# Keeping four engines in program order beside a stream of gathers

## The chip, the cores and the metric

The kernel runs on one core of one Trainium2 chip. The metric is the device time of one execution, in microseconds; lower is better. Each run was timed beside the kernel before on the same chip. The median of the kernel before in the first measurements was 12008.74 us (3 runs; with a fourth, timed beside the changed kernel, 12002.22).

A ratio here is the mean time of one kernel's fast runs over that of the other's in the same rounds. It is therefore not quite the ratio of the medians that are quoted beside it.

## The reference

The input has 4 images of 256 channels and 64 x 64 pixels, in float32. Four layers follow each other, each with a group normalisation in front and a residual sum behind. What matters here is in layer 0:

```python
t = depthwise3x3(y)                                  # per channel
offset, mask = einsum(t, off_w), softmax(einsum(t, mask_w))
sg = 2.0 * (loc + offset / norm) - 1.0               # where to look, 9 points x 4 groups per pixel
samp = _grid_sample(img, sg)                         # bilinear: 4 neighbours of each point
dout = (samp * mask).sum(-1)                         # the "sampling"
dout = einsum(dout, outproj_w) + outproj_b
... # squeeze-excite and a feed-forward of 1024 channels
# layer 1: linear attention with 5x5 depthwise "taps"; layer 2: binarised 3x3 conv; layer 3: attention
```

The sampling reads data-dependent rows of a table in device memory. Everything else is dense arithmetic.

## The kernel before

Each image goes through *prepare*, then *sample*, then *first* (feed-forward and layer 1), then *second* (layers 2 and 3). The sampling of one image runs beside *first* and *second* of earlier images. The sampling is written like this:

```python
RP, UR, BR = 14, 4, 20            # 14 pixels a round, 4 rounds a unit, 20 rounds a block
...
for u in range(0, len(rounds), UR):
    unit = rounds[u:u + UR]
    wm = self.gp.tile([P, UR, 4 * G, OB], F32, name="wm")
    self.tc.keep_in_program_order(nc.vector.tensor_tensor(wm[:, 0:nu], ...))   # weights of the unit
    acc = self.ps1.tile([P, UR, P], F32, name="acc")
    for v, (r, m) in enumerate(unit):
        g = self.gp.tile([P, G, 256], F32, name="g", bufs=10)      # ring of 10 buffers
        for i in range(G):
            nc.gpsimd.indirect_dma_start(out=g[:, i, :], ..., in_=table, ...)   # 4 gathers a round
        for x in range(2):
            for i in range(G):                                     # 8 matmuls a round, 32 columns each
                nc.tensor.matmul(acc[32 * i:32 * i + 32, v, :], wm[:, v, ...],
                                 g[:, i, x * P:(x + 1) * P], start=x == 0, stop=x == 1)
    at = sp.tile([P, UR, P], F32, name="at", bufs=1)
    nc.scalar.copy(at[:, 0:nu], acc[:, 0:nu])                      # accumulator to SBUF
    dp = self.ps1.tile(...)
    for v in range(nu):
        nc.tensor.transpose(dp[:, v]..., at[:, v], self.ident)     # then dT <- dp on ScalarE
    ...
    yield 1                                                        # one step a unit
```

The work beside is a set of Python generators. After each step of the sampling, `beside` advances them by their share of a budget. An order written in this way is only a wish: the framework's scheduler decides at build time how the instructions stand in each engine's queue.

Of the kernel before, what the change touches and what calls it, by code (L numbers as in the profile page):

```python
# [1 line left out]

# [33 lines left out]
PREPARE = NB * 20 + NCH * 45  # L36
FIRST = NB * 28 + 2 * (NB * 10 + NCH * 56) + NB * 8 + NCH * 96
SECOND = 2 * NB * 16 + NB * 6 + NT * 9
# [27 lines left out]
class Net:  # L66
# [34 lines left out]
    def groupnorm(self, pool, st, name):  # L101

        nc = self.nc
        mv = pool.tile([P, KT, 2], F32, name=name + "_mv")
        for k in range(KT):
            nc.vector.bn_aggr(mv[:, k, :], st[:, k].rearrange("p b s -> p (b s)"))
        pg = self.ps(name + "_pg")
        nc.tensor.matmul(pg[:, 0:KT], self.bd8, mv[:, :, 0], start=True, stop=True)
        mg = pool.tile([P, KT], F32, name=name + "_mg")
        nc.vector.tensor_copy(mg, pg[:, 0:KT])  # L110
        d = pool.tile([P, KT], F32, name=name + "_d")
        nc.vector.tensor_tensor(d, mv[:, :, 0], mg, ALU.subtract)
        nc.vector.tensor_tensor(d, d, d, ALU.mult)
        nc.vector.tensor_tensor(d, d, mv[:, :, 1], ALU.add)
        pv = self.ps(name + "_pv")
        nc.tensor.matmul(pv[:, 0:KT], self.bd8, d, start=True, stop=True)
        sc = self.rsqrt(pool, pv[:, 0:KT], EPS_GN, KT, name)
        bi = pool.tile([P, KT], F32, name=name + "_bi")
        nc.vector.scalar_tensor_tensor(bi, mg, -1.0, sc, ALU.mult, ALU.mult)
        return sc, bi  # L120
# [41 lines left out]
    def depthwise(self, acc, src, w, k, rows, cols, r0, bias=None):  # L162

        nc = self.nc
        for t in range(k * k):
# [6 lines left out]
            else:  # L172
                nc.vector.tensor_scalar(acc, s, wt, None, ALU.mult)

# [92 lines left out]
    def prepare(self, n, w, sp, bp):  # L267
# [8 lines left out]
        sc, bi = self.groupnorm(sp, st, "g0")  # L276
# [4 lines left out]
        nc.vector.tensor_scalar(low, sh, SLOPE, None, ALU.mult)  # L281

# [14 lines left out]
        for b in range(NB):  # L297
# [5 lines left out]
            for m in range(KT):  # L303
# [4 lines left out]
                self.spread([p[:, m] for p in pads], rw(yb[:, m]), b, 1)  # L308
            nc.sync.dma_start(self.y_d[n][:, :, b * 512:(b + 1) * 512], yb)
# [5 lines left out]
            for j2 in range(2):  # L315
                ps = self.ps().rearrange("p (j o) -> p j o", o=C)
                for j in range(2):
                    at = (2 * j2 + j) * P
                    for k in range(KT):
                        nc.tensor.matmul(ps[:, j], yb[:, k, at:at + P], w["iw"][:, k], start=k == 0, stop=k == KT - 1)  # L320
                nc.vector.tensor_tensor(xo[:, 2 * j2:2 * j2 + 2, :], ps,
                                        self.row("inproj_b").unsqueeze(1).to_broadcast([P, 2, C]), ALU.add)
            for r in range(2):
# [6 lines left out]
            yield 17 - 2 * (b == 0)  # L330
# [27 lines left out]
    def offsets(self, n, c, y, mw, bp):  # L358
# [3 lines left out]
        for k in range(KT):  # L362
            acc = self.ps1.tile([P, 16, W], F32, name="agg", tag="agg")
            self.depthwise(acc, y[:, k], self.w3[:, k], 3, 16, W, 0, bias=self.sh[:, 2 + k:3 + k])
            nc.scalar.activation(t[:, k], acc.rearrange("p r w -> p (r w)"), AF.Identity, scale=SLOPE)
            nc.vector.tensor_tensor(t[:, k], acc.rearrange("p r w -> p (r w)"), t[:, k], ALU.max)
            yield 14
# [11 lines left out]
        self.coordinates(bp, n, c, off, ml)  # L379
        yield 17  # L380

    def coordinates(self, bp, n, c, off, ml):
# [27 lines left out]
            self.con("gi").rearrange("p (g q) -> p g q", q=PT).unsqueeze(1).to_broadcast([P, CT, G, PT]), ALU.add)  # L410

# [5 lines left out]
        nc.scalar.activation(mg, mg, AF.Exp)  # L417
        nc.vector.tensor_reduce(mx, mg, AX.X, ALU.add)
        nc.vector.reciprocal(mx, mx)
        nc.vector.tensor_tensor(mg, mg, bc(mx), ALU.mult)  # L420
        mf = ml.rearrange("p t q -> p (t q)")
        wt = sd[:, :, :, G:].rearrange("p t q (g a b) -> p t g q a b", g=G, a=2)
        for xt, wx in ((0, w0[:, 0]), (1, loc[:, 0])):
# [6 lines left out]
            sd.rearrange("p t q f -> p t (q f)"))  # L430


    def sample(self, n, ssum):


        nc, sp = self.nc, self.sp2
        table = self.tab[n].rearrange("g y x s c -> (g y x) (s c)")
        for b, (p0, np_) in enumerate(BLOCKS):
            sl = sp.tile([P, BR, G * 5], F32, name="sl")
            whole, part = np_ // RP, np_ % RP  # L440

            nr = whole + (part > 0)
            rows = self.s_d[n][p0 * PT:p0 * PT + nr * RS, :].rearrange("(r p) f -> p r f", p=RS)
# [3 lines left out]
            yb = sp.tile([P, KT, BP], F32, name="yb", bufs=1)  # L447
            nc.sync.dma_start(yb[:, :, 0:np_], self.y_d[n][:, :, p0:p0 + np_])
            dT = sp.tile([P, G, BP], F32, name="dT", bufs=1)
            rounds = [(r, RP) for r in range(whole)] + [(whole, part)] * (part > 0)  # L450
            for u in range(0, len(rounds), UR):
                unit = rounds[u:u + UR]
                nu = len(unit)

                wm = self.gp.tile([P, UR, 4 * G, OB], F32, name="wm")
                sh = [P, nu, 4 * G, OB]

                self.tc.keep_in_program_order(nc.vector.tensor_tensor(  # L458
                    wm[:, 0:nu], self.con("own").unsqueeze(1).unsqueeze(1).to_broadcast(sh),
                    sl[:, u:u + nu, G:].unsqueeze(3).to_broadcast(sh), ALU.mult))  # L460
                acc = self.ps1.tile([P, UR, P], F32, name="acc")
                for v, (r, m) in enumerate(unit):
                    g = self.gp.tile([P, G, 256], F32, name="g", bufs=10)
                    for i in range(G):
                        nc.gpsimd.indirect_dma_start(  # L465
                            out=g[:, i, :], out_offset=None, in_=table,
                            in_offset=bass.IndirectOffsetOnAxis(ap=sl.bitcast(I32)[:, r, i:i + 1], axis=0))


                    for x in range(2):  # L470
                        for i in range(G):
                            nc.tensor.matmul(acc[32 * i:32 * i + 32, v, :], wm[:, v, 4 * i + 2 * x:4 * i + 2 * x + 2, :],  # L472
                                             g[:, i, x * P:(x + 1) * P], start=x == 0, stop=x == 1)
                at = sp.tile([P, UR, P], F32, name="at", bufs=1)
                nc.scalar.copy(at[:, 0:nu], acc[:, 0:nu])  # L475
                dp = self.ps1.tile([P, UR, G, 2, OB], F32, name="dp", tag="dp")
                for v in range(nu):
                    nc.tensor.transpose(dp[:, v].rearrange("p g s o -> p (g s o)"), at[:, v], self.ident)  # L478

                full = sum(1 for _, m in unit if m == RP)  # L480
                for v0, v1, m in ((0, full, RP), (full, nu, unit[-1][1])):
                    for s in range(2):
                        if v0 < v1:
                            hs = slice(64 * s, 64 * s + 64)
                            q0 = RP * (u + v0)
                            nc.scalar.copy(
                                dT[hs, :, q0:q0 + m * (v1 - v0)].rearrange("p g (v o) -> p g v o", o=m),
                                dp[hs, v0:v1, :, s, 0:m].rearrange("p v g o -> p g v o"))
                yield 1
            for m in range(KT):  # L490
                po = self.ps1.tile([P, 512], F32, name="po", tag="dp")
                for k in range(G):
                    nc.tensor.matmul(po[:, 0:np_], self.ow[:, k, m * P:(m + 1) * P], dT[:, k, 0:np_], start=k == 0, stop=k == G - 1)  # L493
                ym = yb[:, m, 0:np_]
                nc.vector.tensor_tensor(ym, po[:, 0:np_], ym, ALU.add)  # L495
                nc.scalar.activation(ym, ym, AF.Identity, bias=self.sh[:, 4 + m:5 + m],
                                     scale=self.inv[:, 4 + m:5 + m], accum_out=ssum[:, m, b:b + 1])
            nc.sync.dma_start(self.x2_d[n][:, :, p0:p0 + np_], yb[:, :, 0:np_])


    def feedforward(self, n, ssum, st):
        nc, tc, a = self.nc, self.tc, self.a
        with tc.tile_pool(name=f"fa{n}", bufs=1, side="right") as sp, \
# [16 lines left out]
            nc.scalar.activation(dn, ps[0:64, 0:1], AF.Relu, bias=self.vec("se_down_b")[0:64])  # L520
            ex = sp.tile([P, KT], F32, name="ex")
# [5 lines left out]
            for k in range(KT):  # L527
                nc.scalar.activation(f1[:, k], f1[:, k], AF.Identity, scale=ex[:, k:k + 1])
            for b in range(NB):
# [3 lines left out]
                for m in range(4 * KT):  # L533
# [4 lines left out]
                    if m % 2:  # L538
                        yield 3.5
                for m in range(KT):  # L540
# [4 lines left out]
                    yield 7  # L545
# [4 lines left out]
    def layer1(self, n, st, st2):  # L550
# [3 lines left out]
        with tc.tile_pool(name=f"la{n}", bufs=1, side="right") as sp, \  # L554
# [5 lines left out]
            sc, bi = self.groupnorm(sp, st, "g1")  # L560
            qb = self.folded(sp, qw, qw, sc, bi, "g1")
            nc.vector.tensor_tensor(qb, qb, self.vec("qkv_s", n=6), ALU.mult)
            nc.vector.tensor_tensor(qb, qb, self.vec("qkv_b", n=6), ALU.add)
            ln = sp.tile([P, 4, P], F32, name="ln")
# [3 lines left out]
            def rows(tiles, seen, cost):  # L568
# [4 lines left out]
                for b in range(NB):  # L573
# [5 lines left out]
                    for i, t in enumerate(tiles):  # L579
# [11 lines left out]
                        else:  # L591
                            self.spread(dst, None, b, 2, lambda own: nc.scalar.activation(own, rw(ps), AF.Relu, **bn))
                    if seen:
                        seen[1](b, got)
                    yield cost
# [4 lines left out]
            def aggregate(pd, i, name, func, **more):  # L600

                acc = self.ps1.tile([P, 16, W], F32, name="agg", tag="agg")
                self.depthwise(acc, pd, self.w5[:, i], 5, 16, W, 0, bias=self.b5[:, i:i + 1])
                v = bp.tile([P, 16, W], F32, name=name, tag="ag", bufs=3)
                nc.scalar.activation(v, acc, func, **more)  # L605
                return v

            for t in range(2):
# [3 lines left out]
                def outer(kind, kv, vv, first, last):  # L612
# [6 lines left out]
                    nc.scalar.copy(kt, pt)  # L619
                    for j in range(2):  # L620
# [3 lines left out]
                def plain(b, kv):  # L624
                    for i in range(2):
                        cs = slice(256 * i, 256 * i + 256)
                        outer(0, kv[0][:, cs], kv[1][:, cs], b + i == 0, b + i == NB)

                sums[0] = self.ps1.tile([P, 2, P], F32, name="vk", tag="vk")
                for got in rows((2 + t, 4 + t), (ks[:, 0], plain), 10):  # L630
# [4 lines left out]
                    ak = fl(aggregate(kp, 2 + t, "ak", AF.Relu, accum_out=ks[:, 1, c:c + 1]))  # L635
                    yield 28
                    av = fl(aggregate(vp, 4 + t, "av", AF.Copy))
                    for i in range(4):
                        cs = slice(256 * i, 256 * i + 256)
                        outer(1, ak[:, cs], av[:, cs], False, c + i == 6)  # L640
                    yield 28
# [320 lines left out]
```

## Time and profile before

| stretch | us before |
|---|---|
| up to the first gather | 262 |
| sampling 1, 2, 3, 4 | 1948, 2194, 2713, 2730 |
| after the last gather (tail) | 2381 |
| profiled span | 12228.0 |

The stretches are counted from the first gather of each image. The prediction shows the slices, the table by stage and the waits. The columns of the view of waits are engine and line, what was waited for, us in total, times, longest. "issue" is time in which the engine waited for nothing that the profile shows, and "remote" stands where it finds no releaser.

```profile
ACT at L475 <- remote: 855.1, 65, 36.3
PE dp L478 <- issue: 350.7, 55, 12.3
```

### The profile page before, as it was taken

What the parts mean: (1) busy time and instruction counts of PE and PEld (TensorE: products, weight loads), DVE (VectorE), ACT (ScalarE), POOL (GpSimd) and SP (SyncE); (2) the same over time, 40 slices, a digit from 0 to 9 for tenths busy, and PEclk for the clock granted to TensorE, in tenths of its full rate; (3) what the DMA queues carried; (4) which work ended last, traced back from release to release, by engine and by line L of the source; (5) the groups of instructions that cost most, each with busy time, mean ns of one, the idle gap of its engine ahead of it and who ended that gap; (6) DMA issues with size and microseconds to landing.
All of it is one profiled execution on the core that took longest, in us unless ns stands there. A gap on an engine that the chain in (4) does not pass through costs nothing. (4 is left out here: it accounts for less than half of the span.)

```text
span 12228.0 us, 90771 instructions
## 1 busy us (share of the span) xinstructions
PE 6881.9 (56%) x35020; PEld 3815.9 (31%) x35020; DVE 5299.1 (43%) x6375; ACT 1843.2 (15%) x3642; POOL 4482.7 (37%) x4694
## 2 busy tenths in 40 slices
PE   3444444573444567655445667655346678545697
PEld 2222222232222223333232333333223334233345
DVE  7333333224654531345453431345453434776613
ACT  1101111111111111111111111111111111121102
POOL 1555656444564543443444333443444310000000
PEclk6666666686666678777666778777666789767799
DMA  5444544332332333332222233332222221100021
GB/s 156 132 133 121 140 120 122 103 101 75 92 98 84 97 100 86 93 90 83 77 81 77 77 96 88 95 89 84 75 81 77 79 74 52 32 26 26 29 59 40
DMA packets 808688, 1052.45 MB, mean 86 GB/s; under 512 B 461248, under 2 KB 515648, under 8 KB 806464
## 3 DMA queue, kind: packets, MB, share of 16 engines
q0 software_dynamic: 225024, 614.77, 17.6%
q1 hardware_dynamic: 583232, 431.88, 12.4%
q8 instruction: 276, 4.52, 0.2%
q14 instruction: 156, 1.28, 0.0%
HBM read 878.36 MB, written 167.90 MB: 86 GB/s over the span
## 5 line engine op out<-in xcount | busy, mean ns | idle before, releaser
L465 POOL DMA_INDIRECT g<-tab,sl x4688 | 4482.1, 956 | 5364.8 <-PE acc L472 3361.0
L169 DVE SCALAR_TENSOR_TENSOR agg<-pad,vec,agg 128x1024 f32<-128x1024 f32 x2560 | 3295.1, 1287 | 85.6 <-ACT pad L356 21.4
L472 PE MATMUL acc<-g,wm 128*32 128x128 f32 x18752 | 1057.4, 327 | 789.9 <-issue 632.7
L478 PE MATMUL dp<-ident,at 128*128 128x128 f32 x1172 | 312.7, 418 | 2007.8 <-issue 1219.0
L472 PEld LDWEIGHTS acc<-g,wm 128*32 128x32 f32 x18752 | 702.9, 130 | 1209.6 <-issue 954.8
L715 PE MATMUL ps<-xp,w 128*128 128x512 f32 x2304 | 1055.8, 611 | 19.9 <-DMA xp<-x 12.1
L478 PEld LDWEIGHTS dp<-ident,at 128*128 128x128 f32 x1172 | 200.6, 208 | 2185.3 <-issue 1348.4
L475 ACT COPY at<-acc 128x512 f32<-128x512 f32 (+1 forms) x296 | 171.9, 581 | 3923.2 <-remote 3587.1
L715 PEld LDWEIGHTS ps<-xp,w 128*128 128x128 f32 x2304 | 442.7, 197 | 542.0 <-issue 520.6
L536 PE MATMUL ps<-x2f,f 128*128 128x512 f32 x1024 | 544.6, 683 | 99.9 <-DVE hm L160 55.7
L160 DVE SCALAR_TENSOR_TENSOR hm<-ps,vec,lk 128x512 f32<-128x512 f32 x256 | 190.6, 750 | 765.9 <-ACT lk L159 645.0
L458 DVE TENSOR_TENSOR wm<-con,sl 128x1024 f32<-128x1024 f32 (+1 forms) x296 | 354.1, 1207 | 308.8 <-remote 274.4
L543 PE MATMUL ps<-hm,f 128*128 128x512 f32 x1024 | 479.5, 623 | 8.7 <-DVE hm L160 6.8
L810 PE MATMUL ps<-gt,pT 128*128 128x128 f32 x2048 | 407.7, 376 | 122.3 <-issue 58.8
L617 PE MATMUL pt<-ident,av 128*128 128x128 f32 x256 | 90.8, 411 | 641.6 <-ACT av L605 629.7
L582 PE MATMUL ps<-xr,qw 128*128 128x512 f32 x768 | 434.1, 702 | 17.5 <-DVE gt L781 10.7
L493 PE MATMUL po<-dT,ow 128*128 128x280 f32 (+1 forms) x960 | 352.6, 525 | 158.4 <-DVE yb L495 85.0
L810 PEld LDWEIGHTS ps<-gt,pT 128*128 128x128 f32 x2048 | 373.7, 280 | 167.4 <-DVE pT L807 79.3
L805 PE MATMUL pt<-ident,pe 128*128 128x128 f32 x1024 | 205.1, 347 | 353.5 <-ACT pe L798 328.3
L171 DVE TENSOR_SCALAR agg<-pad,vec,b 128x1024 f32<-128x1024 f32 x96 | 128.9, 1342 | 597.7 <-ACT pad L352 278.5
L159 ACT ACTIVATE lk<-ps,low 128x512 f32<-128x512 f32 x320 | 217.9, 686 | 973.2 <-PE ps L536 559.0
L536 PEld LDWEIGHTS ps<-x2f,f 128*128 128x128 f32 x1024 | 215.8, 220 | 387.6 <-issue 271.0
(225 smaller groups left out, 7335.8 us busy)
## 6 DMA issues: line engine op xcount, KB each, us to landing
x<-x SPq DMA_DIRECT2D x160, 512.0 KB
g<-tab,sl POOLq DMA_INDIRECT x4688
xr<-x SPq DMA_DIRECT2D x128, 512.0 KB
x<-in_x SPq DMA_DIRECT2D x64, 512.0 KB
tab<-xo SPq DMA_DIRECT2D x512, 64.0 KB
y<-yc SPq DMA_DIRECT2D x32, 512.0 KB
x2f<-x SPq DMA_DIRECT2D x32, 512.0 KB
xyf<-x SPq DMA_DIRECT2D x32, 512.0 KB
```

The source lines that it names most:

```text
L159: nc.scalar.activation(t, ps, AF.Identity, bias=low, scale=SLOPE)
L169: nc.vector.scalar_tensor_tensor(acc, s, wt, acc, ALU.mult, ALU.add)
L458: self.tc.keep_in_program_order(nc.vector.tensor_tensor(wm[:, 0:nu], self.con("own").unsqueeze(1).unsqueeze(1).to_broadcast(sh), sl[:, u:u ...
L465: nc.gpsimd.indirect_dma_start(out=g[:, i, :], out_offset=None, in_=table, in_offset=bass.IndirectOffsetOnAxis(ap=sl.bitcast(I32)[:, r, i: ...
L472: nc.tensor.matmul(acc[32 * i:32 * i + 32, v, :], wm[:, v, 4 * i + 2 * x:4 * i + 2 * x + 2, :], g[:, i, x * P:(x + 1) * P], start=x == 0, ...
L478: nc.tensor.transpose(dp[:, v].rearrange("p g s o -> p (g s o)"), at[:, v], self.ident)
L493: nc.tensor.matmul(po[:, 0:np_], self.ow[:, k, m * P:(m + 1) * P], dT[:, k, 0:np_], start=k == 0, stop=k == G - 1)
L536: nc.tensor.matmul(ps, f1[:, k, m * P:(m + 1) * P], x2[:, k], start=k == 0, stop=k == KT - 1)
L543: nc.tensor.matmul(ps, f2[:, k, m * P:(m + 1) * P], hm[:, k], start=k == 0, stop=k == 4 * KT - 1)
L582: nc.tensor.matmul(ps, qw[:, k, t * P:(t + 1) * P], x[:, k], start=k == 0, stop=k == KT - 1)
L715: nc.tensor.matmul(ps, w[:, k, t, m * P:(m + 1) * P], xp[:, k, t // 3:t // 3 + 8, t % 3:t % 3 + W], start=i == 0, stop=i == KT * 9 - 1)
L810: nc.tensor.matmul(ps[:, 0:P], pT[:, m], gt[:, m], start=m == 0, stop=m == 7)
```

## The change

The intent is that between two rounds of gathers each engine gets a small, equal piece of other work, and that PE, DVE, ScalarE and GpSimd keep that order as it is written. The change has four parts:

1. *Fixed order:* within the samplings the scheduler may not reorder these four engines.
2. *Fine steps:* the generators yield after every few microseconds, and the sampling yields after every round and not after every unit.
3. *Deferred reading:* the transposes and the projection of a unit are put off into later rounds.
4. *Early preparation:* the weights of the next unit and the table of the next block are made one ahead.

```diff
-PREPARE = NB * 20 + NCH * 45
-FIRST = NB * 28 + 2 * (NB * 10 + NCH * 56) + NB * 8 + NCH * 96
-SECOND = 2 * NB * 16 + NB * 6 + NT * 9
+PREPARE = 370
+FIRST = 1590
+SECOND = 612
...
@@ depthwise
+            if t % 5 == 4 or t == k * k - 1:
+                yield 6.5
...
@@ sample
+        wm, later = weigh(0, 0), []
+        for i, (b, u) in enumerate(order):
+            sl, units = blocks[b]
+            acc = self.ps1.tile([P, UR, P], F32, name="acc")
+            for v, (r, _) in enumerate(units[u]):
+                if later:
+                    later.pop(0)()
+                gathered(sl, wm, acc, v, r)
+                if not v and i + 1 < len(order):
+                    if order[i + 1][1] == 0:
+                        load(b + 1)
+                    nxt = weigh(*order[i + 1])
+                if v + 1 < len(units[u]):
+                    yield 1
+            at = sp.tile([P, UR, P], F32, name="at", bufs=1)
+            nc.scalar.copy(at[:, 0:len(units[u])], acc[:, 0:len(units[u])])
+            wm = nxt
+            later.append(partial(turn, units[u], b, u, at))
+            if u + 1 == len(units):
+                later += [partial(project, b, m) for m in range(KT)]
+            yield 1
...
@@ run
+        in_order = {E.PE, E.DVE, E.Activation, E.Pool}
-        beside(self.sample(1, ssum[1]), [(first(0), FIRST)])
+        with self.tc.manual_schedule(engines=in_order):
+            beside(self.sample(1, ssum[1]), rounds, [(first(0), FIRST)])
...      (the other samplings likewise; some 40 further yields are left out)
```

## The prediction

> **What bounds the kernel now.** I began with the page's busy shares: no engine is above PE's 56%, so no engine's work alone sets the time. Next the forty slices:
>
> ```profile
> PE   3444444573444567655445667655346678545697
> DVE  7333333224654531345453431345453434776613
> ...
> POOL 1555656444564543443444333443444310000000
> PEclk6666666686666678777666778777666789767799
> ```
>
> The first line that matters is not a tall one. POOL, which only issues the gathers, runs at 3 to 6 tenths from 262 us to 9848 us and then stops; during all that time nothing else is full. So four samplings, back to back, take 9586 of 12228 us, and a tail without gathers takes 2380 us. Each sampling has 293 rounds (14 blocks of 20 and one of 13) of four gathers, 1172 in all; counting gathers in windows of 250 us gave the four boundaries. Busy times by stage (columns: us of the stretch, then PE, PE's weight loads, DVE, ACT, POOL with instruction counts, granted clock, DMA share, GB/s):
>
> ```profile
> 262.00:2204.00 1942.00, 830.79 (x6048) 513.13 (x6048) 674.25 (x941) 215.43 (x450) 1129.99 (x1167) 0.64 0.47 129
> 2204.00:4397.00 2193.00, 1113.83 (x6749) 601.04 (x6749) 991.98 (x970) 315.51 (x622) 1117.80 (x1172) 0.68 0.33 94
> 4397.00:7117.00 2720.00, 1585.90 (x8355) 873.04 (x8355) 1102.53 (x1281) 421.26 (x841) 1119.05 (x1179) 0.73 0.29 84
> 7117.00:9848.00 2731.00, 1592.27 (x8393) 876.93 (x8391) 1118.07 (x1308) 423.12 (x848) 1114.97 (x1172) 0.73 0.30 85
> 9848.00:12228.00 2380.00, 1652.62 (x5137) 884.87 (x5137) 1222.59 (x1619) 434.08 (x822) 0.12 (x1) 0.82 0.13 41
> ```
>
> Even the last sampling leaves PE idle for 1140 us, DVE for 1610 and POOL for 1616. What POOL waits for there is in the view of its waits (us in total, times, longest):
>
> ```profile
> POOL g L465 <- PE acc L472: 1234.7, 62, 58.4
> POOL g L465 <- issue: 327.5, 1072, 0.6
> ```
>
> A gather needs a free buffer, and the matmul that frees it comes late. Back to back, a gather starts every 1.25 us (0.95 us of work, 0.30 us of issue), so 1172 of them need 1465 us; the rest is PE's lateness. Why PE is late, the timeline shows at one spot (start, duration, engine, instruction, idle time before it):
>
> ```profile
> 8510.13 0.47 PE L617 MATMUL pt<-ident,av 128*128 128x128 f32 x1 [17.41 <-ACT av L605]
> ...
> 8520.26 1.96 PE L472 MATMUL acc<-g,wm 128*32 128x128 f32 x64
> ```
>
> ```profile
> 8521.20 0.94 POOL L465 DMA_INDIRECT g<-tab,sl  x1 [17.36 <-PE acc L472]
> ```
>
> PE stands 17.41 us before a transpose that needs the depthwise taps of DVE; the sampling's matmuls, whose data had landed (no gather had been issued for 17 us), stand behind it in PE's queue, 32 of them in one lump, and POOL stands just as long. The kernel is bound by the order in PE's queue, not by an amount of work.
>
> **What the Trainium skill says.** (1) "TensorE: Matmul & The Clock Gate", Part 3, The mechanism: matmuls start and end strictly in order, without reordering. The spot above agrees: landed data waited 17 us behind a transpose. (2) Same page, Part 1: an idle window of about 3.4 us halves PE's clock. This trace agrees: the clock is 0.73 in the last sampling and 1.00 in 10000 to 10250 us, where PE is busy throughout; so a denser PE also gets shorter matmuls. (3) "Perfetto Trace Analysis", Tensor Engine Instruction: the end of a matmul is an estimate of the profiler. This fits waits that I cannot assign: in the last sampling PE's transpose of the accumulator waits 350.7 us for "issue", though ACT before it waits for PE.
>
> **The change, part by part.** *Removed:* the scheduler's freedom on four engines, within the samplings only. *Added:* no arithmetic; the counts of matmuls are equal in both programs (19,120). *Moved:* in the built order the 32 matmuls of a unit stand in one run 249 times before; after, 668 runs are of 8 (one round), 103 of 16, and other matmuls between two runs are 8 in the median and 16 at the 90th percentile (38 before, with single stretches up to 202). The weights wm are made one unit ahead, the index table one block ahead, and the transposes follow the copy of the accumulator only after other work. So PE gives back buffers round by round, and the ring of 10 buffers (50 us of gathering) can bridge a wait.
>
> *Cost.* The budgets in the diff are in microseconds, nearly: five taps are 6.5 units and 5 x 1.287 us = 6.4 us. Per round the work beside gets 1590/293 = 5.43 units of first, 612/293 = 2.09 of second, 3 x 370/293 = 3.79 of prepare. POOL's floor is 4 x 1.25 = 5.0 us a round. I estimate each stretch by its fullest engine, then add for waits:
>
> - Two works beside (samplings 3 and 4), feed-forward: 328 units, 60 rounds. A full-clock matmul record of 512 columns is 7.03/16 = 0.44 us (timeline, line 715). Feed-forward has 64 records per 40 units, 28.2 us, so 3.8 us a round; layer 2 has 72 per 32 units, 31.7 us, so 2.1; the sampling's own matmuls about 1.1. PE: 7.0 us; with waits 7.2.
> - Taps: 24 x 32.5 = 780 units, 144 rounds. DVE: 738.8 + 32.1 = 771 us over 144 is 5.35, wm 88.6/293 = 0.3, the second work 0.3 to 0.7: 6.0 to 6.4; with waits 6.8.
> - The rest, 89 rounds: the attention's 32 records per 16 units give 4.8, layer 3 about 1.0, the sampling 1.1: 6.9; with waits 7.2.
> - Sum 60 x 7.2 + 144 x 6.8 + 89 x 7.2 = 2052, plus about 50 for filling and draining: 2100 us for each, against 2720 and 2731.
> - First alone (sampling 2): the same without the second work: 60 x 5.4 + 144 x 6.3 + 89 x 6.3 = 1792, with the edges 1840 us, against 2193.
> - Prepare beside (sampling 1): DVE 2.3 us and PE 2.8 us a round are small; POOL's 5.0 plus table writes (DMA share 0.47) makes 5.4, 293 x 5.4 = 1582, taken as 1600 us, against 1942.
> - Before 262 us and after 9848 us no engine's order is pinned; only the finer steps reach the tail. Unchanged: 262 and 2380 us.
>
> Sum: 262 + 1600 + 1840 + 2 x 2100 + 2380 = 10282 us in the profile. Profiled, the kernel before took 12228 us and unprofiled 12008.74, so times 0.982: 10,100 us. The percentages added for waits (3 to 12%) are my choice; no view gives them.
>
> **Rivals.** *Lock-step:* with four queues in one order, an engine that waits holds up all that follows, and waits of PE on ACT, ACT on DVE and DVE on PE add up instead of being bridged; the scheduler could at least lift ready work over them. For it: softmax, num/rden pairs and leaky steps make two or three handoffs inside one step. Against: each step's chain is some 3 to 8 us, its next step comes a round (6 to 7 us) later, and the program breaks steps just at the handoffs. It would leave about 2600 us per double stage, 11,300 to 12,200 in all. *The unassigned waits stay:* if the 350 us before the transposes come from how PE works and not from the order, about 250 us per sampling remain, 11,100. Against: the transposes now stand farther behind. *GpSimd becomes the bound:* if all waits are bridged, four samplings of 1465 us give 262 + 5860 + 2380 = 8502, times 0.982 = 8350. Against: DVE's taps and PE's feed-forward need over 5.0 us a round where they stand, so only the first sampling can get near. *The loads:* SP is not pinned, and its loads wait behind stores that wait for DVE (1519.6 us of SP's waits are line 688 for DVE). A late load now stops a whole queue; 0 to 300 us.
>
> **Range and chances.** A miss of 1 us a round over the 1172 rounds is 1172 us, of which I take 0.6 down and 0.8 up: 9,400 to 11,050. The lower side needs nearly full engines, the upper side a good part of the lock-step. Faster by over 2%: 0.93; within 2%: 0.04; slower: 0.03, which would take lock-step worse than the present order.
>
> **What would show it right or wrong.** Right: POOL's wait for acc in the last sampling falls from 1234.7 us below 600, its digits become even, 5 to 7 tenths; the granted clock in the samplings rises from 0.73 to 0.8 or more; samplings last near 1600, 1840, 2100 and 2100 us; the tail stays at 2380 within 100. Wrong: double samplings above 2500 us, with PE waiting in many short pieces for DVE and ACT (lock-step); the "issue" wait of the transposes unchanged (the second rival); all samplings at 1500 us (the third); DVE or PE waiting for DMA on lines of loads (the last). A tail that moves by more than 100 us would show that the finer steps matter outside the pinned part, which I set to nothing.

## The result, and the profile after

The changed kernel takes 10060.2 us (median of 4 runs, 10048.37 to 10061.98), against 12002.22 us for the kernel before (4 runs, 11975.6 to 12008.78). The ratio is 0.838, with an interval of 0.837 to 0.840. The prediction was 10,100 us.

The slices of the changed kernel, each a fortieth of 10057.6 us, are these:

```profile
PE   4444445577454569966657699665576985456797
...
DVE  7443443423667662256676722567767248866413
...
POOL 0666666666666665555665555556554000000000
PEclk7666666688666779987878899877787997777798
```

GpSimd's digits, which were 3 to 6 and uneven, are now an even 5 to 6, and they end earlier. No engine is full over the whole of a sampling. Busy times by stage (columns as in the prediction: stretch, us, then PE, PE's weight loads, DVE, ACT and POOL with counts, granted clock, DMA share, GB/s):

```profile
266.00:1982.00 1716.00, 814.52 (x6098) 506.73 (x6098) 705.73 (x936) 216.95 (x453) 1155.70 (x1172) 0.65 0.52 146
1982.00:3755.00 1773.00, 1036.26 (x6736) 555.16 (x6735) 996.50 (x967) 313.81 (x621) 1144.68 (x1173) 0.73 0.40 115
3755.00:5737.00 1982.00, 1416.96 (x8311) 776.01 (x8310) 1118.86 (x1292) 411.64 (x835) 1136.07 (x1173) 0.83 0.40 115
5737.00:7738.00 2001.00, 1428.30 (x8401) 783.83 (x8405) 1127.77 (x1311) 418.72 (x849) 1137.60 (x1171) 0.83 0.40 116
7738.00:10057.00 2319.00, 1651.58 (x5141) 880.37 (x5141) 1207.34 (x1610) 435.69 (x826) 1.17 (x2) 0.83 0.14 42
```

The four samplings shrank by 2113 us (9585 to 7472), and the tail by 62. (The profiled execution of the kernel before took 226 us more than the timed ones, 12228.0 against 12002.22, so these differences are somewhat too large.) In the double samplings the granted clock rose from 0.73 to 0.83. The waits in the last sampling answer to the lines in the prediction and to the two shown behind it:

```profile
POOL g L481 <- PE acc L488: 450.0, 108, 16.1
POOL g L481 <- issue: 301.8, 990, 0.6
ACT at L541 <- remote: 166.3, 22, 18.4
PE dp L501 <- issue: 9.6, 3, 6.5
```

The wait for the accumulator's matmuls fell from 1234.7 to 450.0 us, and the longest single wait from 58.4 to 16.1 us. The nameless "issue" wait of the transposes is down to 9.6 us, from 350.7, and that of the copy to 166.3, from 855.1. Here is how PE's queue looks at a spot with the same kind of work (start, duration, engine, instruction, idle time before it):

```profile
6745.18 1.08 PE L488 MATMUL acc<-g,wm 128*32 128x128 f32 x16
6747.02 1.11 PE L501 MATMUL dp<-ident,at 128*128 128x128 f32 x4 [0.76 <-ACT at L541]
6748.07 1.08 PE L488 MATMUL acc<-g,wm 128*32 128x128 f32 x16
...
6752.79 0.88 PE L488 MATMUL acc<-g,wm 128*32 128x128 f32 x16
```

```profile
6763.88 0.94 POOL L481 DMA_INDIRECT g<-tab,sl  x1 [2.30 <-PE acc L488]
```

The accumulator's matmuls come mostly in pieces of one round (8 matmuls of 2 passes make 16 records). In PE's order 54 runs of 64 are left, of 249. GpSimd waits 2.30 us for a buffer there; at the prediction's spot it waited 17.36.

So far everything fits the story of the prediction. The experiments show that it is only half of the story.

### The profile page after: what moved, and what is told of

The parts are those of the page before. It is cut to its first block, busy times and chain, and to the rows that moved or that the text cites. A ratio compares the mean times of both kernels' runs of the same rounds, so it can differ in the third digit from the quotient of the medians.

```text
span 10057.6 us, 90742 instructions
## 1 busy us (share of the span) xinstructions
PE 6455.6 (64%) x35020; PEld 3569.6 (35%) x35020; DVE 5349.4 (53%) x6375; ACT 1830.6 (18%) x3642; POOL 4575.9 (45%) x4694
## 5 line engine op out<-in xcount | busy, mean ns | idle before, releaser
L481 POOL DMA_INDIRECT g<-tab,sl x4688 | 4575.2, 976 | 3162.9 <-issue 1242.4
L488 PEld LDWEIGHTS acc<-g,wm 128*32 128x32 f32 x18752 | 636.8, 129 | 948.8 <-issue 861.0
L501 PE MATMUL dp<-ident,at 128*128 128x128 f32 x1172 | 253.1, 354 | 931.0 <-ACT at L541 636.1
L588 PE MATMUL ps<-x2f,f 128*128 128x512 f32 x1024 | 481.7, 617 | 13.5 <-DVE hm L165 4.6
L868 PE MATMUL ps<-gt,pT 128*128 128x128 f32 x2048 | 363.1, 350 | 142.9 <-DVE pT L864 93.3
L635 PE MATMUL ps<-xr,qw 128*128 128x512 f32 x768 | 393.3, 646 | 27.9 <-DMA xr<-x 26.6
L868 PEld LDWEIGHTS ps<-gt,pT 128*128 128x128 f32 x2048 | 337.3, 257 | 188.0 <-DVE pT L864 117.1
L508 ACT COPY dT<-dp 64x224 f32<-64x224 f32 (+1 forms) x592 | 199.0, 336 | 804.1 <-PE dp L501 425.2
L676 PE MATMUL vk<-kt 128*128 128x128 f32 x1024 | 213.0, 346 | 203.4 <-ACT kt L673 105.8
L596 DVE TENSOR_TENSOR xyf<-xyf,ps 128x512 f32<-128x512 f32 x64 | 44.0, 688 | 550.7 <-PE ps L595 436.0
```

What stands on the lines that cost most here:

```text
L481: nc.gpsimd.indirect_dma_start(out=g[:, i, :], out_offset=None, in_=table, in_offset=bass.IndirectOffsetOnAxis(ap=sl.bitcast(I32)[:, r, i: ...
L488: nc.tensor.matmul(acc[32 * i:32 * i + 32, v, :], wm[:, v, 4 * i + 2 * x:4 * i + 2 * x + 2, :], g[:, i, x * P:(x + 1) * P], start=x == 0, ...
L501: nc.tensor.transpose(dp[:, v].rearrange("p g s o -> p (g s o)"), at[:, v], self.ident)
L588: nc.tensor.matmul(ps, f1[:, k, m * P:(m + 1) * P], x2[:, k], start=k == 0, stop=k == KT - 1)
L635: nc.tensor.matmul(ps, qw[:, k, t * P:(t + 1) * P], x[:, k], start=k == 0, stop=k == KT - 1)
L868: nc.tensor.matmul(ps[:, 0:P], pT[:, m], gt[:, m], start=m == 0, stop=m == 7)
```

## The experiments

The theory to be tested was the prediction's: the gain comes from the order in PE's queue, because the sampling's matmuls no longer stand behind work that waits. The first rival was that the fixed order itself costs time (lock-step) and the gain comes from the finer steps. The second was that PE is late for a reason of its own, which the records do not show. The expectations of the first four runs were written with a kernel before of 12,000 us in mind. The texts of later runs name theories by letters: C is the second rival in a sharp form (matmuls on four groups of 32 columns run one after another), and D is its opposite (they overlap, and the time is lost elsewhere).

### First job, chip 3: the parts of the change alone

The first surprise was the chip. The kernel before took 9386.97 us there (3 runs, 9382.59 to 9394.53), 22% less than in the first measurements, without any change to it. The expected microseconds below are therefore off by this much, and only ratios can be compared.

**e1_unpinned**: the changed program, with the scheduler free on all engines.

```diff
-            with self.tc.manual_schedule(engines=in_order):
+            with nullcontext():          # in both places
...
-            nc.vector.tensor_tensor(wm[:, 0:nu], ...)
+            self.tc.keep_in_program_order(nc.vector.tensor_tensor(wm[:, 0:nu], ...))     # as before
```

> The changed kernel with its order left to the scheduler again on all four engines (only the weights wm keep their place in DVE's order, as in the kernel before); fine steps, the budgets and the deferred transposes stay. Theory A, the order itself is the gain: the scheduler lumps the accumulator's matmuls of a unit again (runs of 32 in PE's queue), GpSimd's wait for them in the fourth sampling goes back above 1000 us, time 11,500 to 12,200. Theory B, the finer steps and the deferred transposes are the gain and the pins add little: below 10,400.

Measured: 9125.99 us, ratio 0.972 (0.969 to 0.975).

**e2_coarse_pinned**: the program of before, unchanged in its steps, with the fixed order.

```diff
-        beside(self.sample(1, ssum[1]), [(first(0), FIRST)])
+        with self.tc.manual_schedule(engines=in_order):
+            beside(self.sample(1, ssum[1]), [(first(0), FIRST)])     # the other samplings likewise
```

> The kernel before with the four engines pinned to its own program order in the samplings: steps as coarse as they were, the work beside follows each unit of four rounds in one lump, and the transposes follow the copy of the accumulator at once. Theory A (the order alone is the gain): 10,000 to 10,500. Theory B (pins need the fine steps, else the queues go in lock-step): PE waits for the copy of the accumulator in every unit and for DVE's 25 taps in one piece of 32 us; double samplings stay above 2400 us, time 11,000 to 12,500.

Measured: 10512.3 us, ratio 1.120 (1.117 to 1.123). GpSimd's wait for the accumulator in the last sampling of this run:

```profile
POOL g L465 <- PE acc L472: 868.9, 57, 37.6
```

**e3_pin_pe_only**: the changed program with only PE in program order.

```diff
-        in_order = {E.PE, E.DVE, E.Activation, E.Pool}
+        in_order = {E.PE}
```

> The changed kernel with PE alone pinned; ACT, DVE and GpSimd are ordered by the scheduler. If the gain comes from where the sampling's matmuls stand in PE's queue (my reading), most of it stays: 10,000 to 10,500. If all four queues have to agree (a scheduler that orders DVE and ACT by its own idea of time makes PE wait for them), 10,700 to 11,800.

Measured: 9246.71 us, ratio 0.985 (0.982 to 0.988).

**e4_no_defer**: the changed program with all four engines fixed, but each unit is transposed and projected at once.

```diff
                 later += [partial(project, b, m) for m in range(KT)]
+            while later:
+                later.pop(0)()
             yield 1
```

> The changed kernel, pinned, but with the transposes and the projection of a unit traced at once after the copy of the accumulator, not one piece a round. My reading of the kernel before says that PE stood before these transposes (491 us in its fourth sampling): then PE's wait before them comes back, 73 units of some 1 to 2 us more each, plus lumps of two projections a block: 100 to 200 us per sampling, time 10,450 to 10,850. If the ring of ten buffers bridges such waits, as GpSimd had 1465 us of work in 2000 us, nothing moves: within 1% of 10,060.

Measured: 9751.09 us, ratio 1.039 (1.036 to 1.042).

What follows: on this chip the fixed order is a cost. It costs 12% on coarse steps (e2). The fine steps with a free scheduler gain 3% (e1), and fixing PE alone takes 1.3 points of this back (e3). Coarse steps in a fixed order (e2) are much worse than fine ones (about 1.005 to 1.008, from e9 on chip 4 below), and reading each unit at once (e4) is worse by 3%, so fine steps and deferred reading are what makes the fixed order bearable. I first read this as a win for the lock-step rival, but none of it explains a gain of 16% elsewhere. So the next job repeated both kernels.

### Second job, chip 10: repeat, and two changes of size

The kernel before took 12232.9 us here (7 runs, 12201.42 to 12256.43): the slower kind again. The first measurements, for which no chip number is recorded, agree with this kind.

**e5_after_again**: the changed kernel, unchanged.

> The changed kernel as it is, again, since in the last job the kernel before took 9387 us and not 12,002. Theory M (the machine of the first measurement made every hand-off between engines dearer, and the change's gain is mostly that such hand-offs no longer hold up the gathers): the kernel before is again near 9390 us here, and the change brings little or nothing, 9150 to 9600 us. Theory S (the first ratio holds everywhere): 0.84 of the kernel before of the same job, so 7870 us if that is 9387.

Measured: 10128.6 us (4 runs), ratio 0.828 (0.826 to 0.830). The samplings took 1738, 1801, 2004 and 2011 us, the tail 2315. The result of the change repeats on this kind.

**e6_before_again**: the kernel before, unchanged, for a second trace.

> The kernel before as it is, for a trace from this job's machine. Theory M: GpSimd's wait for the accumulator's matmuls in the fourth sampling is some hundreds of us instead of 1234.7, the waits without an owner (ACT's copy of the accumulator released by nothing the profile names: 3587.1 us; PE's transposes for issue: 1219.0 us) shrink by more than half, busy times of the engines and the tail of 2380 us stay the same within 3%.

Measured: 12243.85 us (one run; its state alone is unknown, but the 7 runs of the same kernel beside it agree). The samplings took 1956, 2208, 2723 and 2713 us, the tail 2384. These are the stages of the first trace. Between e6 and e5, both on one chip, the samplings shrink by 2046 us (9600 to 7554).

**e7_second_later**: *second* starts 60 rounds into its sampling, so that PE's fullest stretch (feed-forward) has less beside it.

```diff
-                    while spent[j] < i * total / number:
+                    while spent[j] < (i - late) * total / (number - late):
...
-                beside(..., [(first(n - 1), FIRST), (second(n - 2), SECOND)])
+                beside(..., [(first(n - 1), FIRST), (second(n - 2), SECOND, 60)])
```

> The changed kernel with the second work of samplings 3 and 4 beginning 60 rounds after the first, so that feed-forward and layer 2, both PE's work, do not lie over each other. If PE's work bounds those 60 rounds (PE is 95% to 98% busy there at full clock, 6.9 us a round), they fall to about 5.3 us and the later rounds, bound by DVE's taps, grow little: 50 to 90 us less per sampling, 100 to 180 us in all. If the rounds after are as full as those before, within 0.5%.

Measured: 10159.7 us, ratio 0.830 (0.828 to 0.832), with samplings of 1739, 1803, 2019 and 2039 us. I had expected 100 to 180 us less and got none. Moving PE's work from one stretch to another does not help.

**e8_ring6**: 6 buffers for gathered rows instead of 10.

```diff
-            g = self.gp.tile([P, G, 256], F32, name="g", bufs=10)
+            g = self.gp.tile([P, G, 256], F32, name="g", bufs=6)
```

> The changed kernel with 6 buffers for gathered rows instead of 10: 30 us of lead instead of 50. If the lead bridges PE's waits (the longest waits of GpSimd for the accumulator were 16 us), it is under 1% slower. If the ring is in use to its end, GpSimd's wait for the accumulator grows and the time rises by 2% to 5%.

Measured: 10111.45 us, ratio 0.827 (0.824 to 0.829), not different from e5. The prediction said that a ring of ten buffers bridges the waits. Six are as good, so the depth of the ring is not what bounds these samplings.

Now the same kernel had traces from both kinds, and they could be laid side by side. Four things are alike on both: the last packet of a gather ends 2.41 to 2.43 us after the start of GpSimd's instruction in the median (48 packets a gather); instruction packets of the DMA take 0.94 us on chip 10 and 0.93 us on chip 4 in the median; tails are equal (changed kernel, 2315 us in e5 and 2306 in e9 below); and the granted clock takes the values 0.5 and 1.0 alone, so a lower ceiling of the clock is not the difference. One thing is not alike, the hand-over from the last accumulator matmul to the copy that reads it. In the trace of before it looks like this, at the spot that the prediction had shown (the run of 64 passes there is recorded as over at 8520.26 + 1.96 = 8522.22 us). First PE, then ACT:

```profile
8522.91 1.02 PE L582 MATMUL ps<-xr,qw 128*128 128x512 f32 x2
8529.12 1.11 PE L478 MATMUL dp<-ident,at 128*128 128x128 f32 x4 [5.18 <-issue]
```

```profile
8528.48 0.59 ACT L475 COPY at<-acc 128x512 f32<-128x512 f32 x1 [7.69 <-remote]
```

ACT had been idle for 7.69 us, and still it began 6.26 us after the recorded end of what it read. The same program's run of 64 passes on chip 3 (e2), first PE, then ACT:

```profile
6017.84 1.95 PE L472 MATMUL acc<-g,wm 128*32 128x128 f32 x64
```

```profile
6019.86 0.59 ACT L475 COPY at<-acc 128x512 f32<-128x512 f32 x1 [22.68 <-PE acc L472]
```

Here the copy begins 0.07 us after the recorded end, at 6019.79. The table gives the median hand-over where ACT was idle already, by the length of PE's last run of accumulator passes:

| trace | runs of up to 16 passes | runs of 49 and more |
|---|---|---|
| before, first trace | (53 cases, mixed) | 6.25 us (169 cases) |
| before, e6 on chip 10 | (59 cases, mixed) | 6.26 us (171) |
| after, first trace | 1.84 us (119) | (6 cases) |
| after, e5 on chip 10 | 1.95 us (112) | 6.24 us (9) |
| coarse and fixed, e2 on chip 3 | 0.09 us (55) | 0.11 us (240) |

"Mixed" means that other runs stand close ahead of a short one, so that the number is not that of the short run. Summed over the 296 units, the hidden time in front of the copy is 2054 us in the first trace of before and 956 us in that of after, and 30 us in e2. On the slower kind, the result thus comes late by about 0.1 us for each accumulator pass (6.25/64 = 0.098, and 1.9/16 = 0.12). This is a mean; the fourth job below shows how uneven it is. In the Trainium skill, "Perfetto Trace Analysis", section Tensor Engine Instruction, says that a matmul's recorded end is an estimate. Here the copy follows it after about 0.1 us on one chip and after 6.2 us on another.

This gave Theory C: on the slower kind the four column groups of the accumulator run one after another, while the records assume that they overlap. A copy of the kernel with a measurement in front of it could tell.

### Third job, chip 4: a measurement of the column groups

The kernel before took 9384.46 us (7 runs, 9373.88 to 9392.93): the faster kind.

**e9_after_measure**: the changed kernel, with three rows of 256 matmuls in front, whose real end is the start of a copy.

```diff
+            for r in range(256):
+                at, n = {"four": (32 * (r % 4), 32), "one": (0, 32), "full": (0, P)}[kind]
+                nc.tensor.matmul(t[at:at + n, r // 4 % UR, :], self.ident[:, 0:n], self.ones, start=True, stop=True)
+            nc.scalar.copy(got[0:n], t[0:n])
```

> The changed kernel with three rows of 256 matmuls ahead of everything: (four) the accumulator's form, 32 columns, going round the four column groups; (one) the same in one column group; (full) 128 columns. ACT copies each row's output when its last matmul is really done. Theory C, column groups: on the slow kind of machine (kernel before near 12,100 us) the four groups run one after another and not beside each other, so the row 'four' really ends 30 to 60 us after its modelled end (512 passes of 0.11 us, 56 us, instead of 0.03 us, 15 us), as long as 'one' and 'full'; on the fast kind (before near 9390) 'four' ends on its modelled end, 15 to 20 us. Theory D, something about the gathered data or the waits (not the form) delays these matmuls: 'four' ends within 1 us of its modelled end on either kind. The time less the rows, some 150 to 250 us, is the changed kernel's: 10,050 to 10,150 on the slow kind; on the fast kind I expect 9300 to 9600, near the kernel before, as its pins then bridge little.

Measured: 9569.36 us (4 runs), ratio 1.020 (1.018 to 1.022). The rows themselves cost about 113 us (the first gather came at 375.1 and not at about 262) to 140 us (measured in e12). Without them the changed kernel would take about 9,430 to 9,460 us here, 0.5 to 0.8% more than the kernel before. This is an estimate, as no run timed it without the rows. The timeline of ACT shows the ends of the rows:

```profile
20.41 0.58 ACT L243 COPY at<-acc 128x512 f32<-128x512 f32 x1 [17.14 <-PE acc L240]
77.61 0.57 ACT L243 COPY at<-acc 32x512 f32<-32x512 f32 x1 [56.62 <-PE acc L240]
```

The 512 passes over four groups began at 1.4 us, so they took 19 us; those on one group took 56 us. The groups overlap here, by a factor of 3.

**e10_unpinned_again**: e1 once more, on this chip.

> The kernel of e1_unpinned again, beside the changed one. On the fast kind of machine 0.972 of the kernel before, as there. On the slow kind: if pinning is what keeps the slow matmuls from holding up the queues (theory A), 11,000 to 12,000; if the finer steps and the deferred transposes do it (theory B), 9900 to 10,400.

Measured: 9117.45 us (4 runs, 9111.91 to 9126.18), ratio 0.972 (0.970 to 0.974). On the faster kind this version beats both kernels. Waits in the last sampling, first of the fixed order (e9), then of the free one (e10):

```profile
POOL g L492 <- PE acc L499: 475.4, 114, 16.5
...
ACT pe L865 <- DVE mx L861: 227.2, 32, 17.8
```

```profile
POOL g L481 <- issue: 323.5, 1062, 0.3
POOL g L481 <- PE acc L488: 267.6, 50, 39.7
```

The free order has fewer but longer waits of GpSimd for PE, and 208 us less of them in this stage. In the fixed order ACT, DVE and PE wait for each other in short steps, as the lock-step rival said. The wait of ACT for DVE at the same place is far smaller in the free order:

```profile
ACT pe L854 <- DVE mx L850: 45.7, 19, 6.8
```

The stages show the price: samplings of 1509, 1524, 1917 and 1934 us in e9 against 1515, 1529, 1741 and 1750 us in e10. It is 176 and 184 us in the two double samplings and nothing in the others. PE's order is the smaller part of it: on chip 3, fixing PE alone made these two stages 36 and 38 us longer (e3 against e1).

### Fourth job, chip 10: the same on the slower kind

**e11_unpinned_measure**: e10's program with the rows of matmuls in front.

> Changed program without the fixed order on any engine, with three rows of 256 matmuls of 128 columns put before the rest: four 32-column groups in turn, one group only, all 128 columns. On the faster kind of machine the four groups took 20.4 us to the copy that reads them, one group 56.6 us and all columns 57.7 us. Theory C (on the slower kind the four groups run one after another, with the recorded ends too early): if this job meets that kind, the four groups take about as long as one group, 50 to 60 us. Rival D (the slower kind loses its time elsewhere): still about 20 us. For the order itself: if the fixed order is what gives the gain on the slower kind, the four samplings here are clearly longer than the changed kernel's 1738, 1801, 2004 and 2011 us there (over 5%); if it is the fine steps and the deferred reading of the accumulators, they are within 3% of these. On the faster kind the samplings repeat 1515, 1529, 1741, 1750 us and the rows repeat 20, 57 and 58 us, and all of this stays open.

Measured: 11372.27 us (4 runs, 11337.46 to 11377.98), ratio 0.929 (0.926 to 0.932) to a kernel before of 12228.61 us. The samplings took 1831, 2029, 2379 and 2414 us, the tail 2354.

**e12_before_measure**: the kernel before with the same rows in front.

> The kernel before with the same three rows of matmuls put in front (110 to 135 us more, in the part before the first gather). On the faster kind of machine, of which there is no trace of the kernel before yet: stages sum to about 9385 us plus the rows, so samplings of about 1520, 1540, 1840 and 1850 us and a tail of 2380 us, and the copy of an accumulator follows its last matmul at once (median 0.1 us) where on the slower kind it came 6.2 us later. Theory C says that this hand-over differs and that the rest of the waits for the accumulator, 1235 us of GpSimd in the last sampling on the slower kind, shrink to under 500 us with it. On the slower kind: samplings of 1950, 2210, 2720 and 2725 us, and the row of four groups at about 20 us (rival D) or over 50 us (Theory C).

Measured: 12368.19 us, ratio 1.011 (1.008 to 1.014): the rows cost 12368.19 - 12228.61 = 140 us (97 to 172 by the interval of the ratio). The rows' ends on this chip are these:

```profile
20.34 0.58 ACT L236 COPY at<-acc 128x512 f32<-128x512 f32 x1 [16.95 <-PE acc L233]
77.47 0.57 ACT L236 COPY at<-acc 32x512 f32<-32x512 f32 x1 [56.55 <-PE acc L233]
```

They are the numbers of chip 4. So Theory C fell in the form in which I had put it: by themselves, the four groups overlap on chip 10 as well. In the same run, during the samplings, a run of 49 or more passes again hands over 6.25 us late in the median (176 cases), and e11 repeats 6.22 us (64 cases). Whatever makes them late acts only in the samplings. What it looks like can be seen where the records themselves are stretched, in PE's timeline of e12:

```profile
8765.66 0.37 PE L483 MATMUL acc<-g,wm 128*32 128x128 f32 x1 [1.06 <-issue]
8767.06 0.37 PE L483 MATMUL acc<-g,wm 128*32 128x128 f32 x1 [1.03 <-issue]
...
8770.63 0.37 PE L483 MATMUL acc<-g,wm 128*32 128x128 f32 x1 [1.07 <-issue]
8771.33 0.42 PE L483 MATMUL acc<-g,wm 128*32 128x128 f32 x1 [0.33 <-issue]
8772.75 0.37 PE L483 MATMUL acc<-g,wm 128*32 128x128 f32 x1 [1.00 <-issue]
```

Passes that wait for no semaphore start 0.70 or 1.40 us apart, where in a normal run they start within 0.2 us. Of accumulator passes that waited for nothing, 521 started over 0.5 us after the one before in e12, and 632 in e11; there were none in e9 and one in e10. What the samplings have and the rows in front do not have is gathers in flight, real data instead of ones and an identity matrix, and sums over two matmuls.

No run was made to separate these, but the kept traces do. The packed trace holds the times of PE's semaphore updates, which tell when a round's result was really there. The three traces of the kernel before have 315 runs of 64 passes with an update for each of their four rounds. The rounds took 0.69, 0.44, 2.27 and 5.07 us in the median; on chip 3 (e2, 153 runs) they took 0.69, 0.44, 0.44 and 0.44. In all 315 GpSimd was idle in the first round. In ten of them it issued no gather until the end of the run, and there all four rounds kept the pace of chip 3 (2.0 us together), though other transfers kept the DMA engines busy to 63% and more. In the other 305 the four rounds took 3.9 us or more. After the last gather, issued at 9847.17, a run hands over at once in the first trace too (PE, then ACT):

```profile
9856.71 1.96 PE L472 MATMUL acc<-g,wm 128*32 128x128 f32 x64
```

```profile
9858.79 0.58 ACT L475 COPY at<-acc 128x512 f32<-128x512 f32 x1 [1.38 <-PE acc L472]
```

The copy begins 9858.79 - 9858.67 = 0.12 us after the recorded end. These runs too have real data and sums over two matmuls. So on the slower kind these runs are late only when GpSimd issues gathers beside them. Why, and why on some chips only, stays open.

A second trace of it is in the records themselves. Each gather posts 16 semaphore updates. On chips 3 and 4 the traces hold about 99% of them, on chip 10 and in the two first traces only 21% to 34%, while before the first gather and after the last the counts of DMA updates are alike on both kinds. A releaser that the views name within these samplings is therefore less certain. It also leaves a rival: that partly the word of a pass's end is late, and not the pass. The stretched starts above speak for the passes, since these wait for no semaphore.

What e11 settles is the worth of the order on this kind. Without the rows' 140 us, the fine steps with a free scheduler would give about 11,230 us (an estimate from e11 and e12; 11,200 to 11,275 by that interval), and the fixed order gives 10128.6 (e5). The waits of e11's last sampling show where the difference is:

```profile
POOL g L492 <- PE acc L499: 851.3, 76, 66.9
ACT at L552 <- remote: 679.4, 49, 30.1
```

## Why the prediction was right, and where it was not

| | chips 3 and 4 | chip 10 |
|---|---|---|
| before | 9387, 9384 us | 12233, 12229 us |
| fine steps, free order | 0.972, 0.972 | about 0.918 (e11 less 140 us) |
| fine steps, fixed order (the change) | about 1.005 to 1.008 (e9 less the rows) | 0.828 |
| coarse steps, fixed order | 1.120 | not run |

**The total was right; its conversion was not.** The sum of stages was 10282 profile us, and the profiled span was 10057.6. The factor of 0.982 from profiled to unprofiled time was wrong: the changed kernel's profiled run took 10059.39 us and its median is 10060.2. The 1.8% that I took for a cost of profiling was the difference between runs of the kernel before; on chip 10 it takes 12,200 us without a profile too. The sum was 2.2% too high, and the factor happened to cancel that.

**The stages.** Predicted 1600, 1840, 2100, 2100 and a tail of 2380 us; measured 1716, 1773, 1982, 2001 and 2319. The first sampling is the one that I put too low. The step that failed is "POOL's 5.0 plus table writes (DMA share 0.47) makes 5.4" a round: it is 1716/293 = 5.86 on this kind. GpSimd's work and issue were as reckoned (1155.7 + 321.4 = 1477 us, or 5.04 a round). What stood in place of the 0.4 for table writes is mostly 194.1 us of waits without a releaser in that stage (213.9 in e5), 0.66 a round. The view of e9 on chip 4 has no such wait. On chips 3 and 4 a round takes 5.15 to 5.2 us (1509 to 1520 us), and there GpSimd's floor of 1465 us does come into reach. The working by fullest engine held well in the double samplings. Feed-forward ran at about 6.9 us a round (56 to 60 gathers per 100 us) against 7.2 predicted, and the taps at about 6.45 against 6.8. Of the signs that the prediction named, GpSimd's wait (under 600 us) and its even digits came as said. The clock rose to 0.83 in the double samplings only; it is 0.65 and 0.73 in the first two, where PE has less to do.

**"The kernel is bound by the order in PE's queue, not by an amount of work."** This step was half right. The order matters, for spreading the matmuls took GpSimd's wait for them from 1234.7 to 450.0 us; fine steps without the order leave 851.3 (e11). But on this kind of chip PE's work lasts longer than its records show. In the last sampling of before, 74 units with about 6.25 us each make 463 us beside the 1592 recorded. If the changed kernel's passes are as slow, which its hand-overs suggest, PE has about 1428 + 463 = 1891 us of 2001, and would be nearly full. Both numbers are estimates from the hand-over times, and that PE is nearly full is not shown. It could also explain why e7 and e8 moved nothing.

**The rival "the unassigned waits stay"** named the right mechanism: the 350.7 us came with late results of PE on this kind, and not from the order alone. They are absent on chips 3 and 4, where the copies follow their matmuls at once. Its consequence was wrong. With runs of mostly 16 passes instead of 64, less hidden time stands between the last pass and the copy (1.84 us and not 6.25), and the deferred transposes have other work ahead of them. The wait is 9.6 us in the last sampling, though 177 us of it remain in the first. That the change in the lengths of runs causes the gain of the fixed order on chip 10 (e5 against e11) is argued from this, not shown; no run on chip 10 fixed one engine alone.

**The rival "lock-step"** was real but small. On chips 3 and 4, where no hidden time masks it, it costs 360 us in the two double samplings of e9 against e10. In coarse steps it costs 12% (e2). Its form in the prediction, some 2600 us for each double stage, did not come. Nor did late loads: no line of PE or DVE waits more than 12 us in all for a load in any sampling of the trace after, as far as its updates were recorded.

**The tail** moved by 62 us in the first traces (2381 to 2319) and from 2384 to 2315 in e6 and e5. The prediction had said nothing would reach it except the finer steps, and set these to zero, with 100 us of room. With fine steps, e1, e3 and e9 have 2306 to 2322 us and e11 has 2354; with coarse ones, e2 has 2381. So it is the finer steps, or the new budgets that came with them.

**What stays open.** Two things: why the accumulator is late on some chips while gathers are issued, and whether the kernel before is held back on chips 3 and 4 by PE's order, since no trace of it was taken there. The decision between the two versions depends on the chip: on chip 10 the changed kernel is 10% faster than its free-order version, and on chip 4 it is about 3.5% slower (9,430 to 9,460 against 9117 us).

## What to carry to other kernels

Before trusting a cause, time both kernels on more than one chip: the same change was worth 17% on one and nothing on another. Where a consumer starts late although the profile says that its matmul has ended, compare the recorded end with the start of the idle consumer, because the end may be a model. Where semaphore updates are kept, they tell when the result was there. Fix the order of several engines only with fine steps and put-off reading, and try it against a free order: on coarse steps it was 12% slower on chip 3, and on fine ones about 3.5% slower on chip 4 and 10% faster on chip 10.

## What the Trainium skill lacked or had wrong

- In the Trainium skill, "Perfetto Trace Analysis", section Tensor Engine Instruction, says that the end is an estimate that hopefully matches. On chips 3 and 4 it matched within about 0.1 us; on chip 10 the result of a run of 64 accumulator passes came 6.2 us after the recorded end, and 2054 us were hidden in this way over the first trace of the kernel before. The page gives no way to notice this; the start of an idle ACT copy that reads the result is one, the time of PE's semaphore update another.
- "TensorE: Matmul & The Clock Gate", Part 3, Measured speedup vs the span model, gives 3.07 times for four row tiles. Four column groups in our rows gave 56/19, about 3 times, on both kinds of chip, which is near it. It does not say that the overlap or the pace can be lost in a running kernel: on chip 10, during gathers, passes that waited for nothing started 0.70 or 1.40 us apart (521 pauses of over 0.5 us in e12, none in e9), and the fourth round of a run took 5.07 us in the median and not 0.44.
- No page that I looked up tells that chips can differ so much: the same kernel took 9,384 to 9,387 us on two chips and 12,229 to 12,233 us on a third in the fast state, with equal tails, and the traces hold about 99% of the gathers' semaphore updates on one kind and 21% to 34% on the other.
